# Means of the LayerNorms around the FFN: subtracted from the data, or taken out of w1, w2 and w3 once

## The chip, the cores and the metric

The kernel runs on one core of a Trainium2 chip. The metric is the device time of one execution in microseconds (us); the median of the runs counts. The core has five engines that work side by side, each through its own instructions in order: PE (matrix products, with PEld for its weight loads), DVE (vector), ACT (activations), POOL (GpSimd), and SP, which here only issues DMAs.

## The reference

Sixteen sequences (B) of 512 tokens (S) with 128 features (E) go through an attention block with 16 heads and a gated FFN, each between two LayerNorms without gain and offset:

```python
def _layernorm(x, axis=-1, eps=1e-05):
    m = jnp.mean(x, axis=axis, keepdims=True)
    v = jnp.var(x, axis=axis, keepdims=True)
    return (x - m) / jnp.sqrt(v + eps)

def _L0_ffn_ref(x, w1_w, w1_s, ...):
    # _tlin(x, w, s) = einsum('bsi,oi->bso', x, w) * s
    h = silu(_tlin(x, w1_w, w1_s)) * _tlin(x, w2_w, w2_s)        # 128 -> 512
    h = gelu(_tlin(h, h1_w, h1_s), approximate=False)            # 512 -> 512
    h = gelu(_tlin(h, h2_w, h2_s), approximate=False)            # 512 -> 512
    return _tlin(h, w3_w, w3_s)                                  # 512 -> 128

x = L0_attn_x
x = x + _layernorm(_L0_attn_ref(_layernorm(x), ...))
x = x + _layernorm(_L0_ffn_ref(_layernorm(x), ...))
```

In the attention a head's logits are its scores q q^T times a coefficient that depends on whether two tokens fall into the same hash bucket; then softmax and the product with v follow. All data are float32.

## The kernel before

The kernel is written as many small generators (`prep`, `gather`, `scores`, `coeffs`, `logits`, `softmax`, `attend`, `residual`, `added`, `ffn`, `weights` and others). Each yields its steps with an engine, an estimated cost and a rank. A planner, `Order`, plays them through a clock of its own before anything runs: whenever an engine is free there, it takes the ready step with the lowest rank and emits its instructions. What comes out is one fixed order for each engine. A step that is added, removed or priced otherwise can therefore change the order of everything after it. Scores have rank 0 on PE, av and transposes 1, projections 2, the FFN's products 4, so the FFN fills what attention leaves. Buffers are handed out by counted pools: three PSUM banks for scores, three for the FFN, two for the rest, eleven SBUF buffers for logits, two for x1, one for the transposed input of the FFN.

The unit of attention is a head j of a batch; 256 heads run through one stream. For each head:

- SP issues gathers of `ql`, `qr` (the queries as sums of bfloat16 parts) and `bb` (buckets, broadcast).
- For each of four tiles of 128 tokens PE makes scores `sp` (L881), DVE makes the coefficients `co` (L899) and multiplies the two into `l`, with the row maximum into `mxpad` (L934).
- The maxima of two heads go through a DVE transpose (`mt`), DRAM (`md`) and a broadcast (`mb`); POOL subtracts `mb` from `l` (L991, 128x2048), ACT takes the exponential (L996). Five early heads (`BY_ROWS`) do this on ACT and PE instead.
- After four heads `attend` makes their `av` products on PE (L1056), ACT evicts them (`avs`), PE transposes (`op`, L1077), DVE divides (`rd`, `o`).

When the 16 heads of batch b are done, `added` normalizes `o` into `x1 = x + LN(o)`, `norm_transposed` normalizes and transposes x1 into `xnt_f`, and `ffn` runs four layers: `w` (products with w1 and w2, L1208; silu on ACT, product `h` on DVE), two layers `hp` (L1252; gelu on ACT), and `yp` (L1290). `ffn` ends with LN of `yp` and adds x1. FFN(b) may begin when FFN(b-1) has finished its first hp layer. The last batch is handled in two halves of two tiles.

`moments` makes the two numbers that a LayerNorm needs per token, `rs = (var + eps)^-0.5` and `nm = -mean * rs`; `rescale` then writes `rs * x + nm` on ACT, one instruction for each of four tiles. It is used with name o, f and y in every batch:

- for o and f: DVE `bn_stats` and `bn_aggr` (L438, L442), ACT adds eps (`ve`, L458), POOL takes the power (`rs`, L469), DVE makes `nm`, one instruction on 128x1 for each tile (`negate`, L477);
- for y, whose source is PSUM: ACT copies each tile of `yp` to `y` with the sum in an accumulator (L402), the PSUM bank is handed back, ACT squares with the sum as bias and sums again (L412), then the same ve, rs and nm.

`weights` loads w2, w3, w1, h1, h2 with DMAs issued from ACT; w2 and w3 are multiplied by their scales on POOL, the others' scales are loaded by SP and used later by ACT. `activity` fills PE with products of a zero tile (L1396) until the first FFN begins. The inputs' own LayerNorm (name a, and `inputs`) is not touched.

Of the kernel before, what the change touches and what calls it, by code (L numbers as in the profile page):

```python
# [13 lines left out]
F32 = mybir.dt.float32  # L14
# [176 lines left out]
def tile_lsh_attention_ffn(  # L191
# [77 lines left out]
    ident = const.tile([P, P], F32, name="ident")  # L269
    make_identity(nc, ident)  # L270

    mhalf = const.tile([P, B, NT], F32, name="mhalf")
    nc.gpsimd.memset(mhalf, -0.5)
    eps = const.tile([P, 1], F32, name="eps")
    nc.gpsimd.memset(eps, EPS)
    eps3 = const.tile([P, 1], F32, name="eps3")
    nc.gpsimd.memset(eps3, EPS / E**3)

    junk = const.tile([P, E], BF16, name="junk")
    still = const.tile([P, P], BF16, name="still")  # L280
# [58 lines left out]
    def dve(cost, rank, emit):  # L339
        return ("op", "DVE", cost, emit, rank, None)  # L340

    def act(cost, rank, emit, table=None):
        return ("op", "ACT", cost, emit, rank, table)
# [7 lines left out]
    def get(kind):  # L351
        return ("get", kind)
# [34 lines left out]
    def pairs(tiles):  # L387
        return [tiles[i : i + 2] for i in range(0, len(tiles), 2)]

    def moments(src, name, rank, tiles, copy=None):  # L390


        q, n, t0 = name[0], len(tiles), tiles[0]
        rs = p2.tile([P, NT], F32, tag=f"rs{q}", name=f"rs_{name}_{t0}")
        nm = p2.tile([P, NT], F32, tag=f"nm{q}", name=f"nm_{name}_{t0}")
        if copy is not None:

            sums = p2.tile([P, 2, NT], F32, tag=f"su{q}", name=f"su_{name}_{t0}")

            def sum_(ts_):  # L400
                for t in ts_:
                    nc.scalar.activation(  # L402
                        copy[0][:, t, :],
                        src[:, t, :],
                        AF.Identity,
                        scale=ROOT / E,
                        accum_out=sums[:, 0, t : t + 1],
                    )

            def square(ts_):  # L410
                for t in ts_:
                    nc.scalar.activation(  # L412
                        junk,
                        src[:, t, :],
                        AF.Square,
                        scale=-1.0 * E,
                        bias=sums[:, 0, t : t + 1],
                        accum_out=sums[:, 1, t : t + 1],
                    )

            for ts_ in pairs(tiles):
                yield act(1.0, -2, lambda ts_=ts_: sum_(ts_))
            src = copy[0]
            copy[1]()
            for i, ts_ in enumerate(pairs(tiles)):
                if i:
                    od.loose()
                yield act(1.2, -2, lambda ts_=ts_: square(ts_))
            mean, var = sums[:, 0, :], sums[:, 1, :]
            factor, sign = float(E) ** -3, -1.0 / E  # L430
        else:
            st = p2.tile(
                [P, NT, nc.vector.BN_STATS_DIM], F32, tag=f"st{q}", name=f"st_{name}_{t0}"
            )

            def stats(ts_):
                for t in ts_:
                    nc.vector.bn_stats(st[:, t, :], src[:, t, :])  # L438

            def aggr():  # L440
                for t in tiles:
                    nc.vector.bn_aggr(mv[:, t, :], st[:, t, :])  # L442

            for i, ts_ in enumerate(pairs(tiles)):
                if i:
                    od.loose()
                yield dve(0.46, rank, lambda ts_=ts_: stats(ts_))
            mv = p2.tile(
                [P, NT, nc.vector.BN_AGGR_DIM], F32, tag=f"mv{q}", name=f"mv_{name}_{t0}"
            )  # L450
            yield dve(0.175 * n, rank, aggr)
            mean, var, sign, factor = mv[:, :, 0], mv[:, :, 1], -1.0, 1.0
        ve = p2.tile([P, NT], F32, tag=f"ve{q}", name=f"ve_{name}_{t0}")
        span = slice(t0, t0 + n)
        yield act(
            0.22,
            -5,
            lambda: nc.scalar.activation(  # L458
                ve[:, span],
                var[:, span],  # L460
                AF.Identity,
                bias=eps if factor == 1.0 else eps3,
                scale=factor,
            ),
        )
        yield pool(
            0.37 + 0.16 * n,
            0,
            lambda: nc.gpsimd.tensor_tensor(  # L469
                rs[:, span], ve[:, span], mhalf[:, 0, 0:n], op=ALU.pow  # L470
            ),
        )

        def negate():

            for t in tiles:
                nc.vector.tensor_scalar(  # L477
                    nm[:, t : t + 1],
                    mean[:, t : t + 1],
                    sign,  # L480
                    rs[:, t : t + 1],
                    op0=ALU.mult,
                    op1=ALU.mult,
                )

        yield dve(0.07 * n, rank, negate)
        return nm, rs

    def rescale(src, dst, scales, tiles):

        nm, rs = scales

        def emit(ts_):
            for t in ts_:
                nc.scalar.activation(
                    dst(t),
                    src[:, t, :],
                    AF.Identity,
                    bias=nm[:, t : t + 1],
                    scale=rs[:, t : t + 1],  # L500
                )

        for ts_ in pairs(tiles):
            yield act(0.88, -2, lambda ts_=ts_: emit(ts_))
# [18 lines left out]
            halved[name] = p2.tile([P, NT, E], F32, tag=tag, name=name, bufs=1)  # L523
        return halved[name]

    def norm_transposed(src, xnt, name, rank, tiles):

        xn = shared(f"xn{name[0]}", f"xn_{name}")
        scales = yield from moments(src, name, rank, tiles)
        yield from rescale(src, lambda t: xn[:, t, :], scales, tiles)  # L530
        k = yield get(banks)
        yield from turned(xn, xnt, k, bank(k, f"tp_{name}_{tiles[0]}"), tiles)
# [589 lines left out]
    def added(b, tiles, o, xt, x1, k1, xnt, kx, hs):  # L1122
        scales = yield from moments(o, f"o{b}", 1, tiles)
        kb = yield get(banks)
        ybt = bank(kb, f"yb_{b}_{tiles[0]}").rearrange("p (t e) -> p t e", t=NT)
        yield from rescale(o, lambda t: ybt[:, t, :], scales, tiles)
        span = slice(tiles[0], tiles[-1] + 1)
        yield dve(
            0.1 + 0.125 * len(tiles),
            1,  # L1130
            lambda: nc.vector.tensor_tensor(
                x1[:, span], ybt[:, span], xt[:, span], op=ALU.add
            ),
        )
        od.put(banks, kb)
        yield from norm_transposed(x1, xnt, f"f{b}", 1, tiles)
        od.spawn(ffn(b, tiles, x1, k1, xnt, kx, hs))

    def ffn(b, tiles, x1, k1, xnt, kx, hs):
# [161 lines left out]
        if whole:  # L1301
# [7 lines left out]
            1,  # L1309
            tiles,  # L1310
            (y, lambda: od.put(ffn_banks, kb)),
        )
        kn = yield get(banks)
        ybt = bank(kn, f"yn_{b}_{tiles[0]}").rearrange("p (t e) -> p t e", t=NT)
# [20 lines left out]
    def weights():  # L1335


        for layer, (src, scale, nk, n, name) in enumerate((
            (w2_t, w2_s, 1, HID, "w2"),
            (w3_t, w3_s, NC, E, "w3"),  # L1340
            (w1_t, w1_s, 1, HID, "w1"),
            (h1_t, h1_s, NC, HID, "h1"),
            (h2_t, h2_s, NC, HID, "h2"),
        )):
# [9 lines left out]
            if name in ("w2", "w3"):  # L1354
                if name == "w2":
                    kl = yield get(logit_bufs)
                    sc = p1.tile([P, NT, S], F32, tag=kl, name="scale2")[:, 0, :]
                else:
                    sc = const.tile([P, E], F32, name="scale3")
                yield act(  # L1360
                    0.42,
                    LATE,
                    lambda: nc.scalar.dma_start(out=sc, in_=scale.partition_broadcast(P)),
                )
                yield ("rest", 6.0)
                yield pool(
                    nk * n / 420,
                    2,
                    lambda: nc.gpsimd.tensor_tensor(
                        w, w, sc.unsqueeze(1).to_broadcast([P, nk, n]), op=ALU.mult  # L1370
                    ),
                )
                if name == "w2":
                    od.put(logit_bufs, kl)
            else:
                w_sb[name + "s"] = sc = const.tile([P, NC], F32, name=name + "s")
                yield dma(
                    2,
                    2,
                    lambda: nc.sync.dma_start(  # L1380
                        out=sc,
                        in_=scale.rearrange("(c p) -> p c", p=P),
                        allow_slow_non_contiguous=True,
                    ),
                    cost=0.6,
                )
        od.set(loaded)

    def activity():
# [76 lines left out]
```

## Time and profile before

| | before |
|---|---|
| median of 3 runs | 1368.63 us (1368.58 to 1369.19) |
| the profiled execution: its time, its span | 1371.57 us, 1369.8 us |
| instructions | 21290 |
| mean granted clock of PE | 0.989 |
| MB read from and written to HBM | 153.50, 19.13 |
| subtraction on POOL, 128x2048 | 251 times, 4566 ns |
| l on DVE, 128x512 | 1024 times, 680 ns |
| nm_f, nm_y on DVE, 128x1 | 64 times each, 204 and 204 ns |
| hp on PE, 128x512 float32 | 960 records, 596 ns (two records for one product) |

An instruction's recorded duration can overlap the next one's on the same engine, so what an instruction costs a full engine is the distance from its start to the next start. Busy time is the union of the durations. In the groups of waits, "X <- Y: us, times, longest" is idle time of X that ended when Y was done. In the chain of work that ended last, each line is a start, a duration and what ran.

### The profile page before, as it was taken

Reading aid. Unit: us, or ns where it says so; the run is one execution under the profiler, and the core shown is the slowest. Engines: PE = TensorE matmul, PEld = TensorE weight load, DVE = VectorE, ACT = ScalarE, POOL = GpSimd, SP = SyncE. Lnnn points to the kernel's source line nnn. Section 1 sums busy time; section 2 is a strip of 40 time slices with the busy share of each in tenths; the row PEclk is TensorE's granted clock in tenths of the full one; section 3 lists DMA queues with packets and bytes.
Section 4 is the critical chain, followed back from the end, with each engine's and each line's share of the span. In section 5 each row is a group of like instructions: output and inputs, shape, how many; then the busy total and the mean of one; then the engine's idle time right before and its main releaser. Section 6 shows DMA issues by size and latency. Waiting matters only on the chain.

```text
span 1369.8 us, 21290 instructions
## 1 busy us (share of the span) xinstructions
PE 1316.2 (96%) x6008; PEld 568.3 (41%) x6008; DVE 1234.5 (90%) x3992; ACT 1143.8 (84%) x1665; POOL 1197.4 (87%) x317
## 2 busy tenths in 40 slices
PE   9999999999999999999999999999999999999997
PEld 3344334334443443434344344433443343433466
DVE  4999999799998999999999999999999999999220
ACT  2688888889898898889989798988979898888953
POOL 1398989999899998999989999998999999899810
PEclk9999999899999999999999999999999999999999
DMA  4645454444544545454444545554445545443100
GB/s 135 189 140 154 131 151 138 135 129 134 154 113 128 131 133 142 132 142 134 132 123 128 141 133 144 132 143 116 146 124 139 141 132 140 122 122 116 47 8 8
DMA packets 158867, 174.04 MB, mean 127 GB/s; under 512 B 33821, under 2 KB 117277, under 8 KB 158749
## 3 DMA queue, kind: packets, MB, share of 16 engines
q1 hardware_dynamic: 155937, 169.20, 44.3%
q10 hardware_dynamic: 2811, 3.48, 0.8%
q8 instruction: 48, 0.79, 0.2%
q14 instruction: 71, 0.57, 0.2%
HBM read 153.50 MB, written 19.13 MB: 126 GB/s over the span
## 4 chain that ended last, share of the span: by engine, by line
PE 57%; DVE 24%; POOL 6%; issue 6%; DMA 4%; ACT 3%; SPq 0%; ACTq 0%; POOLq 0%; DVEq 0%
PE hp L1252 25%; PE av L1056 13%; DVE l L934 12%; PE sp L881 10%; DVE co L899 8%; POOL l L991 6%; PE w L1208 3%; DMA mb<-md 2%; PE yp L1290 2%; PE op L1077 2%; DMA bb<-bkd 1%; ACT l L996 1%; PE vp L794 1%; PE activity L1396 1%; DVE h L1178 1%
## 5 line engine op out<-in xcount | busy, mean ns | idle before, releaser
L991 POOL TENSOR_TENSOR l<-l,mb 128x2048 f32<-128x2048 f32 x251 | 1135.6, 4566 | 56.8 <-DMA mb<-md 41.5
L934 DVE CUSTOM_DVE_ANT_0 l<-co,sp 128x512 f32<-128x512 bf16 x1024 | 662.4, 680 | 14.5 <-PE av L1056 11.0
L996 ACT ACTIVATE l<-l 128x2048 f32<-128x2048 f32 x251 | 477.8, 1907 | 23.3 <-POOL l L991 22.1
L1252 PE MATMUL hp<-h,h 128*128 128x512 f32 (+1 forms) x1088 | 494.3, 570 | 0.1
L899 DVE TENSOR_SCALAR co<-bb,bj 128x516 bf16<-128x516 bf16 x1024 | 451.7, 471 | 2.8 <-DMA bb<-bkd 2.8
L881 PE MATMUL sp<-qr,ql 72*128 72x512 bf16 x1024 | 357.8, 384 | 35.6 <-DVE mxpad L934 31.8
L1252 PEld LDWEIGHTS hp<-h,h 128*128 128x128 f32 x1088 | 201.4, 190 | 160.3 <-issue 137.7
L1056 PE MATMUL av<-l,vaug 128*32 128x512 f32 x2008 | 265.1, 605 | 0.0
L881 PEld LDWEIGHTS <-ql 72*128 72x128 bf16 x1024 | 94.6, 98 | 331.8 <-issue 309.6
L1208 PE MATMUL w<-xnt_f,w 128*128 128x512 f32 (+1 forms) x272 | 133.1, 585 | 4.3 <-ACT a L1196 2.6
L996 ACT ACT_TABLE_LOAD x87 | 111.6, 1283 | 1.5
L1056 PEld LDWEIGHTS av<-l,vaug 128*32 128x32 f32 x2008 | 45.7, 109 | 116.6 <-issue 85.2
L1396 PE MATMUL activity<-still 128*128 128x512 bf16 x328 | 88.8, 387 | 1.0 <-DVE still L281 1.0
L934 DVE DVE_READ_ACCUMULATOR2_ANT mxpad<- 128x1 f32 x1004 | 83.0, 83 | 0.0
L1070 ACT COPY avs<-av 128x512 f32<-128x512 f32 x64 | 37.4, 584 | 48.3 <-PE av L1056 48.2
L1266 ACT ACT_TABLE_LOAD x59 | 75.7, 1283 | 1.0
L1208 PEld LDWEIGHTS w<-xnt_f,w 128*128 128x128 f32 x272 | 50.9, 195 | 51.1 <-issue 20.8
L1178 DVE TENSOR_TENSOR h<-w,a 128x512 f32<-128x512 f32 (+1 forms) x68 | 44.2, 656 | 29.4 <-PE w L1208 18.9
L1290 PEld LDWEIGHTS yp<-w,h 128*128 128x128 f32 x512 | 65.7, 193 | 11.3 <-issue 6.7
L1290 PE MATMUL yp<-w,h 128*128 128x128 f32 x512 | 66.5, 277 | 0.0
L469 POOL TENSOR_TENSOR rs_y<-ve_y,mhalf 128x4 f32<-128x4 f32 (+1 forms) x17 | 16.7, 985 | 48.4 <-ACT ve_y L458 47.8
L1266 ACT ACTIVATE h<-hp,h1s 128x512 f32<-128x512 f32 (+1 forms) x68 | 41.8, 660 | 14.9 <-PE hp L1252 14.5
(102 smaller groups left out, 1008.4 us busy)
## 6 DMA issues: line engine op xcount, KB each, us to landing
mb<-md SPq DMA_DIRECT2D x251, 256.0 KB
bb<-bkd SPq DMA_DIRECT2D x256, 130.5 KB
ql<-qd SPq DMA_DIRECT2D x256, 72.0 KB
qr<-qd SPq DMA_DIRECT2D x255, 72.0 KB
qd<-q SPq DMA_DIRECT2D x96, 128.0 KB
xta<-in_L_attn_x_dram SPq DMA_DIRECT2D x16, 256.0 KB
xtr<-in_L_attn_x_dram SPq DMA_DIRECT2D x16, 256.0 KB
xtm<-in_L_attn_x_dram SPq DMA_DIRECT2D x15, 256.0 KB
```

Source lines behind the costliest of these rows:

```text
L881: nc.tensor.matmul(sp, lhsT=ql[:, ts(t, P)], rhs=qr, start=True, stop=True)
L899: nc.vector.tensor_scalar(co, bb.rearrange("p (r c) -> p r c", c=BP)[:, :, 0:BC], bjs[b][:, c : c + 1], float(NBKT - 2), op0=ALU.is_equal, ...
L934: nc.vector.tensor_tensor_reduce(out=l, in0=co[:, 0:S], in1=sp, scale=1.0, scalar=-3.0e38, op0=ALU.mult, op1=ALU.max, accum_out=mx[:, t : ...
L991: lambda: nc.gpsimd.tensor_tensor(l, l, mb.unsqueeze(1).to_broadcast([P, NT, S]), op=ALU.subtract),
L996: yield act(1.82, 0, lambda: nc.scalar.activation(l, l, AF.Exp, scale=SCALE), "exp")
L1056: nc.tensor.matmul(av[k * Q : (k + 1) * Q, :], lhsT=va[:, t, c : c + Q], rhs=ls[gg * GH + k][0][:, t, :], start=(t == 0), stop=(t == NT - 1),)
L1178: lambda: nc.vector.tensor_tensor(h[:, c, cols], g2, a, op=ALU.mult),
L1208: lambda: nc.tensor.matmul(gp, lhsT=w_sb[which][:, 0, ts(c, P)], rhs=xnt[:, cols], start=True, stop=True),
L1252: lambda i=i: nc.tensor.matmul(hp, lhsT=w[:, i, ts(c, P)], rhs=hin[:, i, cols], start=(i == 0), stop=(i == NC - 1),),
L1266: nc.scalar.activation(h[:, c, cols], hp, AF.Gelu, scale=sc[:, c : c + 1])
L1290: nc.tensor.matmul(yp[:, ts(t, E)], lhsT=h[:, i, ts(t, P)], rhs=w_sb["w3"][:, i, :], start=(i == 0), stop=(i == NC - 1),)
L1396: nc.tensor.matmul(bk, lhsT=still, rhs=still.unsqueeze(1).to_broadcast([P, NT, P]), start=start, stop=stop,)
```

## The change

A LayerNorm's mean is constant over a token's 128 features. Subtracting it from the input of w1 and w2 is the same as subtracting, from each column of the two weights, that column's mean over the 128 input features. Subtracting it from the output of w3 is the same as subtracting, from each row of w3, its mean over the 128 output features. The change does this with the weights once:

- `centering` = identity - 1/128. After w2 is scaled and after w1 is loaded, PE multiplies each by it into an FFN bank (`c_w2`, `c_w1`) and ACT copies the result back over the weight.
- w3: DVE sums its rows (`sums3`), scales the sums by -1/E, and ACT adds them as a bias, chunk by chunk.
- w1 is loaded before w3 instead of after it; `centering` and w3's scale share one buffer.
- `moments` has a flag `free`, set for f and y: nm is neither allocated nor made, and `rescale` has bias 0.0. For f the statistics are made as before, mean included, since the variance needs it.
- for y, whose mean is now zero, the four copies with sums become one copy of all tiles, and the squares have no bias; `ve` uses 1/E and eps instead of scaled ones.

```diff
+    centering = p1.tile([P, P], F32, tag="w3", name="centering")
+    nc.vector.tensor_scalar(centering, ident, -1.0 / E, None, op0=ALU.add)
...
-    eps3 = const.tile([P, 1], F32, name="eps3")
-    nc.gpsimd.memset(eps3, EPS / E**3)
...
-    def moments(src, name, rank, tiles, copy=None):
+    def moments(src, name, rank, tiles, copy=None, free=False):
...
-        nm = p2.tile([P, NT], F32, tag=f"nm{q}", name=f"nm_{name}_{t0}")
+        if not free:
+            nm = p2.tile([P, NT], F32, tag=f"nm{q}", name=f"nm_{name}_{t0}")
         if copy is not None:
-            sums = p2.tile([P, 2, NT], F32, tag=f"su{q}", name=f"su_{name}_{t0}")
-            def sum_(ts_):
-                for t in ts_:
-                    nc.scalar.activation(copy[0][:, t, :], src[:, t, :], AF.Identity,
-                        scale=ROOT / E, accum_out=sums[:, 0, t : t + 1])
+            var = p2.tile([P, NT], F32, tag=f"su{q}", name=f"su_{name}_{t0}")
+            mean, factor, sign = None, 1.0 / E, None
             def square(ts_):
                 for t in ts_:
-                    nc.scalar.activation(junk, src[:, t, :], AF.Square, scale=-1.0 * E,
-                        bias=sums[:, 0, t : t + 1], accum_out=sums[:, 1, t : t + 1])
+                    nc.scalar.activation(
+                        junk, copy[0][:, t, :], AF.Square, accum_out=var[:, t : t + 1]
+                    )
-            for ts_ in pairs(tiles):
-                yield act(1.0, -2, lambda ts_=ts_: sum_(ts_))
-            src = copy[0]
+            whole = slice(t0, t0 + n)
+            yield act(
+                0.12 + 0.1 * n, -2, lambda: nc.scalar.copy(copy[0][:, whole], src[:, whole])
+            )
...
+        if free:
+            return None, rs
         def negate():
...
-                    bias=nm[:, t : t + 1],
+                    bias=0.0 if nm is None else nm[:, t : t + 1],
...
-        yield from norm_transposed(x1, xnt, f"f{b}", 1, tiles)
+        yield from norm_transposed(x1, xnt, f"f{b}", 1, tiles, free=True)
...
             (w2_t, w2_s, 1, HID, "w2"),
+            (w1_t, w1_s, 1, HID, "w1"),
             (w3_t, w3_s, NC, E, "w3"),
-            (w1_t, w1_s, 1, HID, "w1"),
...
-                    sc = const.tile([P, E], F32, name="scale3")
+                    sc = p1.tile([P, E], F32, tag="w3", name="scale3")
...
+                else:
+                    sums = const.tile([P, nk], F32, name="sums3")
+                    yield dve(0.6, 2, lambda: nc.vector.reduce_sum(sums, w, axis=AX.X))
+                    yield dve(0.1, 2, lambda: nc.vector.tensor_scalar(
+                        sums, sums, -1.0 / E, None, op0=ALU.mult))
+                    for i in range(nk):
+                        yield act(0.35, LATE, lambda: nc.scalar.activation(
+                            w[:, i], w[:, i], AF.Identity, bias=sums[:, i : i + 1]))
...
+            if nk == 1:
+                kb = yield get(ffn_banks)
+                cp = bank(kb, f"c_{name}")
+                yield pe(1.2, 3, lambda: nc.tensor.matmul(
+                    cp, lhsT=centering, rhs=w[:, 0, :], start=True, stop=True))
+                yield act(0.6, LATE, lambda: nc.scalar.copy(w[:, 0, :], cp))
+                od.put(ffn_banks, kb)
```

More of the change, by code (lines that the diff above doesn't have):

```diff
@@ L388, in pairs @@
         return [tiles[i : i + 2] for i in range(0, len(tiles), 2)]
-    def moments(src, name, rank, tiles, copy=None):
+    def moments(src, name, rank, tiles, copy=None, free=False):
         q, n, t0 = name[0], len(tiles), tiles[0]
         rs = p2.tile([P, NT], F32, tag=f"rs{q}", name=f"rs_{name}_{t0}")
-        nm = p2.tile([P, NT], F32, tag=f"nm{q}", name=f"nm_{name}_{t0}")
+        if not free:
+            nm = p2.tile([P, NT], F32, tag=f"nm{q}", name=f"nm_{name}_{t0}")
         if copy is not None:
-            sums = p2.tile([P, 2, NT], F32, tag=f"su{q}", name=f"su_{name}_{t0}")
-            def sum_(ts_):
-                for t in ts_:
[L402 to L408, printed above, removed]
+            var = p2.tile([P, NT], F32, tag=f"su{q}", name=f"su_{name}_{t0}")
+            mean, factor, sign = None, 1.0 / E, None
             def square(ts_):
@@ L412, in square @@
                     nc.scalar.activation(
[L413 to L418, printed above, removed]
-                    )
-            for ts_ in pairs(tiles):
-                yield act(1.0, -2, lambda ts_=ts_: sum_(ts_))
-            src = copy[0]
+                        junk, copy[0][:, t, :], AF.Square, accum_out=var[:, t : t + 1]
+                    )
+            whole = slice(t0, t0 + n)
+            yield act(
+                0.12 + 0.1 * n, -2, lambda: nc.scalar.copy(copy[0][:, whole], src[:, whole])
+            )
             copy[1]()
@@ L428, in moments @@
                 yield act(1.2, -2, lambda ts_=ts_: square(ts_))
-            mean, var = sums[:, 0, :], sums[:, 1, :]
-            factor, sign = float(E) ** -3, -1.0 / E
         else:
@@ L461, in moments @@
                 AF.Identity,
-                bias=eps if factor == 1.0 else eps3,
+                bias=eps,
                 scale=factor,
@@ L524, in shared, with norm_transposed @@
         return halved[name]
-    def norm_transposed(src, xnt, name, rank, tiles):
+    def norm_transposed(src, xnt, name, rank, tiles, free=False):
         xn = shared(f"xn{name[0]}", f"xn_{name}")
-        scales = yield from moments(src, name, rank, tiles)
+        scales = yield from moments(src, name, rank, tiles, free=free)
         yield from rescale(src, lambda t: xn[:, t, :], scales, tiles)
@@ L1311, in ffn @@
             (y, lambda: od.put(ffn_banks, kb)),
+            free=True,
         )
@@ L1374, in weights @@
                     od.put(logit_bufs, kl)
+                else:
+                    sums = const.tile([P, nk], F32, name="sums3")
+                    yield dve(0.6, 2, lambda: nc.vector.reduce_sum(sums, w, axis=AX.X))
+                    yield dve(
+                        0.1,
+                        2,
+                        lambda: nc.vector.tensor_scalar(sums, sums, -1.0 / E, None, op0=ALU.mult),
+                    )
+                    for i in range(nk):
+                        yield act(
+                            0.35,
+                            LATE,
+                            lambda: nc.scalar.activation(
+                                w[:, i], w[:, i], AF.Identity, bias=sums[:, i : i + 1]
+                            ),
+                        )
             else:
@@ L1386, in weights @@
                 )
+            if nk == 1:
+                kb = yield get(ffn_banks)
+                cp = bank(kb, f"c_{name}")
+                yield pe(
+                    1.2,
+                    3,
+                    lambda: nc.tensor.matmul(
+                        cp, lhsT=centering, rhs=w[:, 0, :], start=True, stop=True
+                    ),
+                )
+                yield act(0.6, LATE, lambda: nc.scalar.copy(w[:, 0, :], cp))
+                od.put(ffn_banks, kb)
         od.set(loaded)
```

## Prediction

> **What bounds the kernel now.** I read the page first, then the busy time by stretch, then the waits of each engine inside the steady stretch, and last the chain at the end. The page's first part:
>
> ```profile
> PE 1316.2 (96%) x6008; PEld 568.3 (41%) x6008; DVE 1234.5 (90%) x3992; ACT 1143.8 (84%) x1665; POOL 1197.4 (87%) x317
> ```
>
> These are averages over three stages: a start of some 130 us without FFN work, a long middle of like batches, and an end of some 75 us with FFN work alone. The busy time by stretch separates the middle (450 to 1240 us, ten batches) from the end:
>
> ```profile
> 450.00:1240.00 790.00, 770.39 (x3482) 321.34 (x3479) 775.79 (x2510) 689.52 (x859) 762.18 (x194) 1.00 0.48 134
> 1296.00:1370.00 74.00, 65.03 (x307) 46.95 (x305) 10.68 (x47) 35.84 (x93) 5.13 (x7) 0.97 0.02 8
> ```
>
> The columns are PE, PEld, DVE, ACT, POOL, then clock and DMA. In the middle DVE is busy 98%, POOL 96.5%, PE 97.5%, ACT 87%: three engines are within two per cent of each other. The waits in the same stretch say who waits for whom (total us, times, longest):
>
> ```profile
> PE sp L881 <- DVE mxpad L934: 17.6, 50, 1.0
> ```
> ```profile
> POOL rs_f L469 <- DVE mxpad L934: 9.1, 3, 3.4
> POOL rs_f L469 <- ACT ve_f L458: 6.3, 3, 2.8
> ```
> ```profile
> DVE rd L1087 <- PE op L1077: 8.6, 11, 1.4
> ```
>
> PE waits for DVE twice as long as DVE waits for PE; POOL waits for the statistics that pass through DVE and ACT. So DVE sets the pace of attention by a narrow margin. The powers of the o-statistics start at 132.49 us (batch 0) and 1238.21 us (batch 14): 79.0 us a batch.
>
> Is PE really nearly full? Its starts answer better than its busy share: in the timeline four hp records from 462.62 are followed by sp at 464.34, so 0.43 us each with nothing between; sp takes 0.22. Per batch 64 hp records, 16 w, 64 sp, four av groups at 3.6 us, yp, transposes and projections sum to about 73 us of the 79, and the changes between sp and av cost some 3 more. The chain at the end:
>
> ```profile
> 1276.24 4.57 POOL l L991
> ...
> 1286.70 13.74 PE hp L1252 x32
> 1300.44 3.57 PE av L1056 x32
> ...
> 1330.53 27.89 PE hp L1252 x128
> 1358.43 3.58 PE yp L1290 x32
> ```
>
> POOL ends its last subtraction at 1295.2 (timeline: two from 1286.22, 9.01 together); after that the last av (1300.4) and 58 us of PE almost without a hole follow, then 7.8 us of the last LayerNorm and its write. What is still queued on PE behind the last av is therefore paid in full.
>
> A rule speaks for a larger gain than I forecast. The Trainium skill, Perfetto Trace Analysis, section Identifying the Most-Contended Engine, takes occupancy for Vector, Scalar and GpSimd, judges TensorE by MFU and LDWEIGHTS busy share instead of matmul share, and says to optimize the most-contended engine first. By it PE (41% in weight loads) has much room, DVE binds alone, and the change would give the whole 13.7 us worked out below, about 1354.9. The starts 0.43 us apart say that PE has little room, and I go by them.
>
> **The change part by part.** The sum is made on the profiled execution: 1371.57 us, span 1369.8, 1.8 outside it; the median of the runs is 1368.63, 2.9 lower. I carry the difference over to the median.
>
> *DVE, removed:* per batch two groups of four nm operations (f and y; o keeps its own). The timeline shows what one costs when DVE is full:
>
> ```profile
> 705.64 0.68 DVE L934 CUSTOM_DVE_ANT_0 l<-co,sp 128x512 f32<-128x512 bf16 x1
> 706.24 0.08 DVE L934 DVE_READ_ACCUMULATOR2_ANT mxpad<- 128x1 f32 x1
> 706.24 0.58 DVE L477 TENSOR_SCALAR nm_f<-mv_f,rs_f 128x1 f32<-128x1 f32 x4
> 706.73 0.47 DVE L899 TENSOR_SCALAR co<-bb,bj 128x516 bf16<-128x516 bf16 x1
> ```
>
> Four take 0.58 recorded but hold the engine 0.49 (706.24 to 706.73), so 0.98 a batch; 14 batches lie before the last o: 13.7 us on the engine that paces. This is the upper end of the gain. The lower end is what the new order itself shows: when the av of head group 60 (of 64) starts, the built program has 510.8 us of FFN products (0.86 a product of 512 columns) behind it instead of 516.9, so at least 6.1 us of PE work leave the attention stage. POOL must follow: it idles 27.8 us of the 790, and 15.4 of that is the rs_f wait above, which a shorter DVE queue shortens. DVE being the fullest, I stand nearer the upper end: 11 us.
>
> *ACT:* per batch four Identity with accumulator from yp become one copy. They start 0.25 to 0.26 us apart (1324.15, .42, .67, .92), 1.0 in all; a 128x512 copy from PSUM takes 0.58 (the avs row). 0.4 us less on an engine 87% busy: hidden by POOL and DVE, at nothing. If ACT were full it would be 6 us. The squares and rescales keep their count. The f and y chains lose a hop through DVE; both are hidden by PE's queued work except for the very last y, below.
>
> *Start:* centering (one 128x128 DVE operation) stands while DVE waits for POOL's power: nothing. PE gets c_w2 between the first transposes and qp, which opens the chain to the first gathers:
>
> ```profile
> 10.47 1.95 PE L644 MATMUL qp<-xnt_a,wq_sb 128*128 128x512 f32 x2 [0.22 <-ACT xnt_a L515]
> ```
>
> c_w2 has qp's shape; it takes the place of one activity product (0.43), so qp is 0.4 (0.86 at full pitch) to 1.5 us late (qp's own 1.95): I take 1.5, the row of the same moment. w1s on SP goes between two qd writes, in a hole of 0.4 us. The eviction of c_w1 (0.58) and three w3 loads stand on ACT ahead of the first qr issue; behind them wait the first scores. In return three h1 loads (256 KB each) leave the place where the first bb landed slowly (5.92 us from 21.24 in the chain): at the 204 to 228 GB/s of that stretch the 768 KB are up to 3.6 us of traffic. They go behind w3's additions and meet the first mb instead, for which POOL waits there anyway (20.67 us before 41.45). w3's sums are one reduction over 128x512 and one small operation on DVE, 0.26 (block) to 0.68 (x) plus 0.2, taken 0.8, standing ahead of head 0's last l and waiting for POOL's scaling of w3; four bias additions (0.48 each) on an idle ACT. Together -3 to +4 us; the terms I can price cancel: 0.
>
> *End:* the order of the built program shows what the quicker attention leaves over. Behind the last av stand 29 hp products of 512 columns instead of 16, all else equal: 13 x 0.86 = 11.2 us. Between the last sp and the last av PE has 19.7 us of work instead of 25.7. From POOL's end to the kernel's end before: 1369.8 - 1295.2 = 74.6. After: 3.5 to the last av (exp 1.9, its table load and hand-overs), 3.6 av, 67.2 queued products (56.0 + 11.2), 0.5 of stalls, and 7.1 for the last y (7.8 less 0.6 for nm and its wait, less 0.15 for copy against two sums): 81.9, so +7.3.
>
> *Sum:* 0 - 11 + 7.3 = -3.7: profiled 1367.9, median 1364.9.
>
> **The rivals.** *PE takes all of it.* Three engines at 96 to 98%: the FFN put off in the middle is done at the end, the total of PE's work is unchanged (two small products more), and only its idle time can shrink. For it: the back-to-back starts and a chain that is 57% PE. Against: the 17.6 us in which sp waits for DVE, which should shrink. Attention 7.3 us quicker, end 7.3 longer: 1368.6.
>
> *The end wins.* The 13 extra products behind the last av cost 7.3 us; this decides as soon as POOL's last subtraction comes less than 7.3 us earlier than 1295.2. POOL runs almost without a hole from 1200 to 1295, and its waits before that are for DMA and ACT as well; if those stay and only 3 us come off, the time is 1368.6 - 3 + 7.3 = 1372.9.
>
> *Start.* The later qp and the crowded first mb give +4 with everything else as forecast: 1368.9, inside the first rival. That the change does not do what it says I exclude: the built program has 24 rows that write nm on DVE instead of 58.
>
> **How the numbers follow.** Forecast 0.47 (1357 to 1365.9), no change 0.22, end wins 0.31. About 0.2% (2.7 us) is what a measurement of this kernel tells from no change; the forecast's band lies under it, so faster 0.47, same 0.22, slower 0.31. Ends of the range: -13.7 - 3 + 5 = -11.7, 1357; -6.1 + 4 + 8.5 = +6.4, 1375. The 5 and 8.5 are the end term with an av that comes 2.3 us before or 1.2 us after my placing.
>
> **What would show it.** Right: rs_o of batch 14 starts 8 to 13 us before 1238.21; sp's wait for DVE under 17.6 in the same ten batches; POOL's last l ends near 1284; from there 80 to 84 us to the end, with hp between the two last av groups fewer and behind them more. Wrong: a batch period of still 79 us (then DVE did not pace); POOL's end before 1280 (then PE had more room than its starts say); a first co much off 27.26 us (then the start decides); a granted clock unlike that of before, which was 0.92 between 212 and 293 us and 1.00 from 450 to 1240, since PE has little room to make up for it.

## The result, and the profile after

The changed kernel took 1379.24 us (median of 4 runs, 1377.11 to 1381.8), the kernel before 1368.91 beside it: a ratio of 1.0072 (95% interval 1.0052 to 1.0093), so about 10 us slower. 1364.9 was forecast, with 1357 to 1375 around it. The profiled execution took 1379.33 us with a span of 1377.5 (before 1369.8): 7.7 us are to be found in the traces. The rest of the 10 is scatter: the traced execution before is 2.7 us over its median. It is one of the late ones, with its first FFN product w at 154.2 us. Six traces whose order up to there is that of before (this one and five of the runs below) have it between 151.0 and 154.9.

The first part of the page after, and the busy time of the same two stages as before (PE, PEld, DVE, ACT, POOL, then granted clock, DMA share and GB/s):

```profile
PE 1323.3 (96%) x6014; PEld 572.2 (42%) x6014; DVE 1222.3 (89%) x3867; ACT 1121.1 (81%) x1560; POOL 1197.3 (87%) x316
```
```profile
450.00:1240.00 790.00, 768.12 (x3446) 318.78 (x3445) 763.76 (x2414) 668.33 (x783) 760.68 (x193) 0.99 0.49 133
1296.00:1378.00 82.00, 73.77 (x325) 50.16 (x323) 9.91 (x36) 36.09 (x85) 5.12 (x7) 0.97 0.04 14
```

The operations are gone as announced: DVE has 125 instructions less, ACT 105. In the middle DVE is busy 12.0 us less and PE 2.3 us less, at a clock of 0.99 instead of 1.00. All three engines that were nearly full are now less full, and the kernel is slower: somebody waits more. From the first FFN product to the last l, before (154.2 to 1271.2) and after (156.0 to 1271.8), the busy times are:

```profile
154.20:1271.20 1117.00, 1081.96 (x4855) 447.44 (x4855) 1086.03 (x3503) 979.73 (x1294) 1071.30 (x269) 0.99 0.48 133
156.00:1271.80 1115.80, 1079.12 (x4823) 444.67 (x4823) 1072.55 (x3385) 955.51 (x1200) 1076.40 (x271) 0.98 0.49 133
```

The waits of DVE in these stretches, before and then after; each line is us, times, longest:

```profile
DVE l L934 <- PE av L1056: 11.0, 6, 3.3
DVE rd L1087 <- PE op L1077: 10.1, 16, 1.4
DVE h L1178 <- PE w L1208: 3.1, 6, 1.3
DVE l L934 <- PE sp L881: 2.8, 8, 0.8
```
```profile
DVE l L924 <- PE av L1046: 13.8, 12, 3.2
DVE rd L1077 <- PE op L1067: 10.7, 14, 1.5
DVE l L924 <- PE sp L871: 9.7, 20, 1.6
DVE h L1168 <- PE w L1198: 4.0, 5, 2.6
```

With the lines under 1 us the sums are 28.2 and 39.1. That closes the account of the engine that paced: from first w to last l it is 1117.0 us before and 1115.8 after; without waits 1088.8 and 1076.7, so 12.1 us less work. (By the rows above it is 13.5 less busy and 12.3 more idle; the list leaves out the shortest waits.) That 12.1 is near the 13.7 computed is partly luck, because three pairs of co and l, some 3 us, now lie ahead of the first w. But 10.9 of it came back as waiting, nearly all of it for scores, av and w on PE, and the first w was 1.8 us later, less than the 3.9 over which it scatters. The last l therefore ends 0.6 us later than before (1271.8), where the forecast wanted it 11 earlier.

In the steady stretch the waits that the prediction named stand so:

```profile
PE sp L871 <- DVE mxpad L924: 18.7, 42, 1.1
...
POOL l L981 <- DMA mb<-md: 16.4, 12, 2.8
...
POOL rs_f L456 <- ACT ve_f L445: 2.1, 1, 2.1
```

PE's wait for DVE did not shrink (17.6 before). POOL's 15.4 us for the statistics of f are nearly gone (2.1), but it waits 16.4 us for the broadcast maxima mb instead of 3.9, and is idle 29.3 us of the 790 instead of 27.8. POOL ends 19.0 us behind the last l instead of 24.0: at 1290.8 instead of 1295.2. The end follows in the chain that ended last:

```profile
1289.81 1.28 ACT L1186
1291.85 2.07 PE w L1198 x2
1293.92 3.24 PE hp L1242 x6
1297.16 3.57 PE av L1046 x32
...
1339.15 26.33 PE hp L1242 x122
...
1368.70 1.76 PE yp L1280 x12
```

From POOL's end to the end of the span it is 86.7 us, 12.2 more than before (74.5). So the 7.7 us are, but for rounding: +0.6 at the last l, -5.0 from there to POOL's end, +12.2 behind it.

### The profile page after: what moved, and what is told of

Its sections match the earlier page's. It is cut to its first block, busy times and chain, and to the rows that moved or that the text cites. A ratio compares the mean times of both kernels' runs of the same rounds, so it can differ in the third digit from the quotient of the medians.

```text
span 1377.5 us, 21072 instructions
## 1 busy us (share of the span) xinstructions
PE 1323.3 (96%) x6014; PEld 572.2 (42%) x6014; DVE 1222.3 (89%) x3867; ACT 1121.1 (81%) x1560; POOL 1197.3 (87%) x316
## 4 chain that ended last, share of the span: by engine, by line
PE 71%; DVE 18%; DMA 3%; issue 3%; ACT 3%; SPq 1%; POOL 0%; POOLq 0%; ACTq 0%; DVEq 0%
PE hp L1242 27%; PE av L1046 16%; PE sp L871 13%; DVE l L924 9%; DVE co L889 6%; PE w L1198 5%; PE yp L1280 4%; PE activity L1417 2%; DMA bb<-bkd 2%; PE op L1067 1%; PE qp L634 1%; PE vp L784 1%; PE pp L673 1%; DVE mxpad L924 1%; DMA xta<-in_L_attn_x_dram 0%
## 5 line engine op out<-in xcount | busy, mean ns | idle before, releaser
L924 DVE CUSTOM_DVE_ANT_0 l<-co,sp 128x512 f32<-128x512 bf16 x1024 | 663.4, 678 | 26.8 <-PE av L1046 13.8
L1198 PE MATMUL w<-xnt_f,w 128*128 128x512 f32 (+1 forms) x272 | 138.1, 601 | 4.1 <-ACT a L1186 3.7
L1280 PEld LDWEIGHTS yp<-w,h 128*128 128x128 f32 x512 | 67.2, 196 | 16.6 <-issue 12.0
```

The lines of the kernel that those rows point to most:

```text
L924: nc.vector.tensor_tensor_reduce(out=l, in0=co[:, 0:S], in1=sp, scale=1.0, scalar=-3.0e38, op0=ALU.mult, op1=ALU.max, accum_out=mx[:, t : ...
L1198: lambda: nc.tensor.matmul(gp, lhsT=w_sb[which][:, 0, ts(c, P)], rhs=xnt[:, cols], start=True, stop=True),
L1280: nc.tensor.matmul(yp[:, ts(t, E)], lhsT=h[:, i, ts(t, P)], rhs=w_sb["w3"][:, i, :], start=(i == 0), stop=(i == NC - 1),)
```

## The experiments

Theory: DVE paces, and what it gained was lost because the planner dealt out another order, in which PE serves attention later and leaves more FFN to the end. Rivals: the centred weights, or the work of centring them, cost time themselves; PE takes all of it; the granted clock falls with the data.

**Is it the data?** The change in its own order, with nothing centred:

```diff
-  sums, sums, -1.0 / E, None, op0=ALU.mult
+  sums, sums, 0.0, None, op0=ALU.mult
-  cp, lhsT=centering, rhs=w[:, 0, :], ...
+  cp, lhsT=ident, rhs=w[:, 0, :], ...
```

> The changed kernel with the identity in the place of the centering matrix and w3's sums multiplied by 0 instead of -1/E: every instruction stays where it is, but w1 keeps its values -1, 0, 1 and w2 and w3 their scaled ones (the means are subtracted nowhere). Theory D (the denser mantissas of the centred w1 make PE draw more, and the granted clock falls): the clock returns to about 0.989, no reduced stretch between 450 and 1290 us, and the time to 1368 to 1371. Theory O (the new order costs the time, and the clock follows the order or chance): 1377 to 1381, clock near 0.982.

Measured: 1377.86 us, ratio 1.0068 (1.0045 to 1.0090). The same loss, and from 230 us on the stretches of reduced clock begin where the change has them, within 2 us. The other way round, the kernel before with dense numbers in the place of w1, and of h1 and h2:

```diff
- in_=src[i * P : (i + 1) * P, :]
+ in_=x[i].rearrange("(p t) e -> p (t e)", t=NT) if name in ("w1",) else src[...]   # or ("h1", "h2")
```

> The kernel before, with 128x512 numbers of the input x loaded into w1 instead of the ternary weight; order and instructions are those of before. Theory D: reduced clock in the middle as after the change, clock 0.98 to 0.985, time up by 4 to 10 us to 1373 to 1379. Theory O: clock 0.989, time 1368 to 1370.

> The kernel before, with numbers of x loaded into h1 and h2, whose products are four times those of w1 and w2 together: the dose of theory D. Theory D: clock 0.94 to 0.975, time 1385 to 1420. Theory O, or a clock that does not look at data: 1368 to 1371, clock 0.989.

Measured: 1368.33 (0.9996; 0.9985 to 1.0007) and 1368.59 (0.9989; 0.9979 to 0.9999), granted clock 0.990 in both. What the weights hold is worth nothing here.

**What is DVE's relief worth by itself?** The kernel before with nm of f and y not issued and the rescales without bias, while the planner still counts the step, so that the order stays:

```diff
- yield dve(0.07 * n, rank, negate)
+ yield dve(0.07 * n, rank, (lambda: None) if free else negate)
...
-     bias=nm[:, t : t + 1],
+     bias=0.0 if nm is None else nm[:, t : t + 1],
```

> The kernel before with the nm operations of f and y not issued and the rescales without bias, while the planner keeps a step of the same cost in their place, so that every other instruction stands where it stood (the mean of f and y is not subtracted). It measures what 13.7 us less on DVE are worth in an unchanged order. Forecast's view (DVE paces by a narrow margin): 1356 to 1362, POOL's last subtraction 8 to 12 us earlier. Rival (PE takes all of it): 1366 to 1369, with DVE's idle time up by what was removed.

Measured: 1360.91 us, ratio 0.9932 (0.9917 to 0.9946): -9.3 us. The last l ends at 1257.8, 13.4 earlier than in the trace of before. Of this 2.8 us is the first w (151.4 instead of 154.2), which lies within its scatter, and 10.6 is the stretch from there to the last l:

```profile
151.40:1257.80 1106.40, 1076.19 (x4853) 446.01 (x4853) 1075.09 (x3395) 969.27 (x1292) 1070.91 (x270) 0.99 0.48 134
```

In the trace of before, the 27 groups of nm in this stretch hold DVE for 13.4 us, from the first start of a group to the next start behind it. The relief earns 10.6 of them. PE's wait for DVE shrinks as the prediction wanted it of the change, while POOL's waits for the statistics of f stay (17.6 us):

```profile
PE sp L882 <- DVE mxpad L935: 14.1, 35, 1.0
...
POOL rs_f L470 <- DVE mxpad L935: 10.3, 3, 3.5
POOL rs_f L470 <- ACT ve_f L459: 7.3, 3, 3.1
```

The counter-test is to relieve PE instead, by one of the 32 hp products of 512 columns in each whole batch, 12.9 us in all:

```diff
- lambda i=i: nc.tensor.matmul(hp, ...)
+ (lambda: None) if layer == 2 and c == 3 and i == 1 and whole else lambda i=i: nc.tensor.matmul(hp, ...)
```

> The kernel before with one of the 32 hp products of each whole batch left out (layer 2, column block 3, second partial product) while the planner still counts it: 15 x 0.86 = 12.9 us less on PE, every other instruction where it stood. It is the mirror of the run without nm (13.7 us less on DVE gave 8.6 to 9.3). If DVE paces attention (forecast's view): 1366 to 1369, POOL's last subtraction within 3 us of 1295. If PE takes all of it: 1356 to 1361.

Measured: 1366.18, ratio 0.9976 (0.9963 to 0.9990): -3.3 us, a quarter. A later run with 20.6 us less on PE (below) gave nothing. So the kernel before gains far more from relieving DVE than PE; "PE takes all of it" falls.

**Is it the order?** The whole change, but played by the planner as the kernel before: the skipped steps still count at their old prices, and the centring is emitted in one piece behind the last weights step.

```diff
+ for i, ts_ in enumerate(pairs(tiles)):
+     yield act(1.0, -2, (lambda: None) if i else lambda: nc.scalar.copy(...))
...
- if free:
-     return None, rs
...
- yield dve(0.07 * n, rank, negate)
+ yield dve(0.07 * n, rank, (lambda: None) if free else negate)
```

> The whole change, computed as the change does it, but with the planner shown the steps and prices of before (empty steps where something is gone), and the centering of w1, w2 and w3 emitted with the last planned step of the weights: two more products on PE, otherwise before's order. If only the order was wrong (theory O): 1357 to 1363, like the run without nm, one or two us more for the centering or one less for the shorter last y. If the weights' part itself costs what the change lost: over 1368.

Measured: 1361.98 us (6 runs, 1360.76 to 1365.32), ratio 0.9950 (0.9938 to 0.9962). The same arithmetic as the change, 17 us quicker than it, and quicker than both kernels. Its waits of DVE from first w to last l:

```profile
DVE l L924 <- PE av L1046: 12.3, 6, 3.3
DVE rd L1077 <- PE op L1067: 10.9, 18, 1.4
DVE h L1168 <- PE w L1198: 2.1, 6, 0.7
DVE l L924 <- PE sp L871: 1.8, 6, 0.6
```

Together with the small ones 29.1, as before (28.2), where the change has 39.1: the wait for sp is 1.8 instead of 9.7. Behind the last av stand 16 hp products, not 29.

Which part of the change disturbs the order? Its FFN half alone (no nm, one copy of yp; weights as before), and its weights half alone (centred, nm kept):

```diff
 # FFN half: the change without its weights part
-            (w1_t, w1_s, 1, HID, "w1"),          # back behind w3
-                    sums = ...; yield dve(...); yield act(...)
-            if nk == 1:
-                ... c_w1, c_w2
 # weights half: the kernel before, with those lines, nm and the four copies kept
```

> One part of the change, planned: f and y without nm, y with one copy, but w1, w2 and w3 untouched as before (the mean is subtracted nowhere). The built order leaves 32 hp products of 512 columns behind the last av (before 16, after the change 29). Theory O: the end after POOL's last subtraction is 85 to 90 us, the time 1372 to 1384 although DVE has 13.7 us less. If the weights' part had spoiled the change: 1356 to 1362.

> The other part, planned: w1, w2 and w3 centred once as in the change, and nm still made and used as before, so that no work is saved. 25 hp products stand behind the last av. Theory O: 1370 to 1380, mostly in the end and in the places of reduced clock. If only the FFN part's order hurts: 1368 to 1371.

Measured: 1382.78 (1.0104; 1.0089 to 1.0119) and 1386.55 (1.0123; 1.0110 to 1.0136). Each alone loses more than both together (0.7%), and with the order kept both together lose nothing, so neither part carries a cost of that size of its own. The second is over the range that I had expected. The barest form changes no instruction at all, only the price that the planner believes for nm:

```diff
- yield dve(0.07 * n, rank, negate)
+ yield dve(0.1225 * n, rank, negate)
```

> The kernel before with one number of the planner changed: the price of negate, 0.07 us a tile, set to the 0.1225 that the trace shows. Not one instruction more or less, another order; 28 hp products behind the last av. Theory O: the order alone moves the time by some 5 to 12 us, here up, 1372 to 1381. If the order matters little and it was the work: 1367 to 1371.

Measured: 1386.30, ratio 1.0122 (1.0107 to 1.0136). Moving the same instructions about costs 17 us, more than I had expected. The order of the kernel before looks like a fortunate one, and a change that re-deals it loses that. To compare under another order, both kernels got another price for ve:

```diff
- 0.22,
+ 0.285,
```

> The change with one price of the planner altered (ve on ACT 0.285, as the trace has it, instead of 0.22): same instructions, another order, 32 hp products behind the last av. Theory O: 1375 to 1390, from POOL's end to the end 85 to 95 us. If the change's order is no accident but its work: 1377 to 1381.

> The kernel before with the same price altered (ve 0.285 instead of 0.22): same instructions, another order, 32 hp products behind the last av. Theory O: well above before, 1378 to 1392, and above the change with the same price by what DVE saves (5 to 13 us). If before's order is not special: 1367 to 1372.

Measured: the change 1376.10 (1.0038; 1.0026 to 1.0049), the kernel before 1384.04 (1.0096; 1.0079 to 1.0113). Under this price the change is 7.9 us ahead. With the order kept it is 8.0 ahead (against 1370.02 of the kernel before beside it). That the two agree so closely is partly luck, since under the new price each kernel still has an order of its own. But all three re-dealt orders without nm of f and y (the change, its FFN half, and this one: 1376.1 to 1382.8) are quicker than all three with it (the weights half and the kernel before under either price: 1384.0 to 1386.6).

**Can the end be bought back?** The change, with the FFN of batch 12 ranked ahead of av and projections, so that less is left over:

```diff
- 4,
+ (0.5 if 12 <= b < 13 else 4),
```

> The change with one rank altered: the FFN products of batch 12 get 0.5 on PE instead of 4. Up to that batch the order is that of the change; at the end 16 hp products of 512 columns stand behind the last av instead of 29. If the backlog at the end is a cost of the change's order (theory O): the time from POOL's last subtraction to the end falls from 86.7 to 74 to 78 us and the whole to 1367 to 1373. If the backlog does not matter, or comes back as a later POOL: 1377 to 1381.

Measured: 1392.52, ratio 1.0156 (1.0136 to 1.0177), far from the 1367 to 1373 that I had expected. The tail behind POOL is back at 74.8 us, and 16 products stand behind the last av, but attention pays: 16 heads that take 77.2 us in the change took 105.3 (DVE from 1127.2 to 1232.5), with DVE busy 78 of the 105:

```profile
1127.00:1232.00 105.00, 93.60 (x380) 40.50 (x382) 77.97 (x244) 76.74 (x97) 79.99 (x22) 0.90 0.37 101
```
```profile
DVE l L924 <- PE av L1046: 35.4, 13, 21.6
```

One wait for av is 21.6 us long. The backlog was moved, not removed: done as one block it stands in front of av, done at the end it is paid behind POOL.

**What halves the clock?** In the change 41.0 us between the first w and the last yp run at a granted clock of 0.50 (before 23.9), in pieces of 3.4 or 6.8 us; the kernel before has none between 431 and 1365, the change five there. Most pieces begin behind a stretch of 3.4 us in which PE had less than half its fill of products (counts in the last section). Around 885 us of the change, the busy time by stretch:

```profile
882.05:885.45 3.40, 1.79 (x8) 0.86 (x8) 3.40 (x13) 2.93 (x5) 3.40 (x2) 1.00 0.04 9
885.50:892.30 6.80, 5.97 (x12) 2.75 (x12) 5.66 (x19) 4.80 (x5) 6.80 (x3) 0.50 0.53 157
```

And its timeline of PE (start, us, operation, in brackets the idle time and who ended it):

```profile
884.32 0.38 PE L871 MATMUL sp<-qr,ql 72*128 72x512 bf16 x1 [1.10 <-DVE mxpad L924]
...
887.30 1.91 PE L1198 MATMUL w<-xnt_f,w 128*128 128x512 f32 x2
889.00 1.91 PE L634 MATMUL qp<-xnt_a,wq_sb 128*128 128x512 f32 x2
890.71 1.06 PE L871 MATMUL sp<-qr,ql 72*128 72x512 bf16 x2
```

No FFN product stands between the sp there, so PE waits for DVE (1.10 us) and is busy 1.79 of 3.40. Right behind, w and qp take 1.70 from start to start instead of 0.86, and DVE waits 1.14 us for the sp behind them before its next l (891.38). To see whether the hole is the cause or only stands beside the dip: 24 of the 32 hp products of FFN(8) are left out of the kernel before, at a place without a dip, against 24 products spread over twelve batches:

```diff
- lambda i=i: nc.tensor.matmul(hp, ..., stop=(i == NC - 1))
+ (lambda: None) if whole and b == 8 and i else lambda i=i: nc.tensor.matmul(
+     hp, ..., stop=(i == NC - 1 or (whole and b == 8)))
# spread: (lambda: None) if whole and 2 <= b < 14 and layer == 2 and c == 3 and i in (1, 2) else ...
```

> The kernel before, its order kept, with 24 of the 32 products of FFN(8)'s two hidden layers left out (of each four that are summed only the first is made): 24 x 0.86 = 20.6 us of PE work missing in one place, between that batch's w (801 us before) and its yp (878 us). The output of batch 8 is therefore not the reference's. Theory W (windows of 3.41 us in which PE runs at most half full are what halves the granted clock next): the share of PE falls to about 0.6 there, single windows to under 0.5, and one or more stretches at clock 0.50, each a multiple of 3.41 us long, begin behind such windows between 824 and 878 us, where the kernel before has none from 427.1 to 1365.7; products inside are 0.85 instead of 0.43 a record. Time: 20.6 us of PE relief at the rate of the run with 15 products less (3.3 us for 12.9) is -5.3, less 2 to 5 us for each dip: 1364 to 1372. Rival (the clock falls for a reason that lies elsewhere in the order or in the time since the start): no dip there, clock 1.00 from 450 to 1240 as before, and about 1364.

> The kernel before, its order kept, with the same number of products left out, 24, but two in each of the twelve batches 2 to 13 (layer 2, last column group, second and third of the four that are summed): the outputs of these batches are not the reference's. 1.7 us of PE work missing in one place at a time. Theory W: single windows lose 1.7 of 3.41 us only where PE would have been full, so few or no new stretches at clock 0.50 between 450 and 1240 (none to two); time by the rate of the run with 15 products less, 0.256 x 20.6 = -5.3: about 1364. Rival (the amount of PE work in the whole kernel moves the clock): the reduced clock is as long as in the kernel with the 24 products left out in one batch. If DVE paces alone and PE's relief is worth nothing, 1368 to 1369 in both.

Measured: with the hole in one place three dips appear where the kernel before has none, at 829.7 (3.4 us), 846.7 (10.2) and 867.2 (6.8); the holes spread out give none between 427 and 1279, but one at 1279.9 (3.4 us), where the kernel before has none either. The kernel with the hole, then the kernel before, in the same stretches:

```profile
820.00:880.00 60.00, 49.32 (x218) 15.97 (x215) 58.74 (x196) 52.86 (x57) 60.00 (x16) 0.83 0.52 134
843.30:846.70 3.40, 1.03 (x3) 0.19 (x2) 3.40 (x15) 2.43 (x3) 3.40 (x2) 1.00 0.82 244
846.75:856.95 10.20, 8.53 (x17) 2.49 (x20) 10.20 (x35) 7.79 (x10) 10.20 (x4) 0.50 0.37 100
```
```profile
820.00:880.00 60.00, 59.22 (x267) 23.17 (x264) 58.99 (x196) 53.06 (x57) 60.00 (x16) 1.00 0.50 134
```

PE is busy 1.03 of 3.40 us, and then the clock is 0.50. So a hole in one place makes dips. The times are 1369.01 (ratio 1.0002; 0.9992 to 1.0011) and 1368.65 (0.9999; 0.9990 to 1.0008): the dips cost nothing that the times show, and DVE ran full through them (58.74 of 60). 20.6 us less on PE earn nothing either. The -5.3 that I expected of the spread holes, by the rate of the run with 15 products less, did not come. In its trace the stretch from first w to last l is 1113.7 us, against 1115.5 to 1117.0 in three traces of the order before with nothing left out (the kernel before and the two with dense weights), but behind POOL's end stand 76.1 us instead of 74.5, with the dip at 1279.9 ahead of it. Between a quarter and nothing, what PE's relief is worth stays open.

## Why the prediction was wrong, point by point

- *DVE, removed, 13.7 us:* the amount was right. With the order kept it earned 10.6 us between first w and last l, and 9.3 of the time, so the 11 would have been about right in the old order. *DVE paces by a narrow margin* is right too, against the rival in which PE takes all: 20.6 us less on PE earned nothing. Its reason was weaker than I read it: in those ten batches DVE's waits for PE sum to 12.5 us, of which I had counted the largest group (8.6), so PE waited 1.4 times as long and not twice.
- *"I stand nearer the upper end: 11 us"* is the step that failed. It sized what attention gains by DVE's work, and priced the new order at nothing but its end. I held the 6.1 us of PE work that leaves the stage for a lower bound; it was none. In the new order DVE waits 10.9 us more for PE, and the last l came 0.6 us late. The batch period (rs_o of batch 0 at 135.18, of batch 14 at 1243.35) stayed at 79.2 us. I had written that a period of 79 would mean that DVE did not pace; that inference was wrong as well: the same relief in the old order shortened it from 79.0 to 78.2. A pace can stay because the pacing engine is given new waits. Why the new order serves scores and av later at each place is not shown beyond the dips below.
- *"POOL must follow"*, since a shorter DVE queue would shorten its wait for rs_f: not so. In the old order that wait stayed (17.6 us after 15.4). In the change it went with the order, and the wait for mb took its place.
- *The clock:* I had named a granted clock unlike before's as what would make the forecast wrong, but put no price on it. The extra dips come from holes in PE, and these from where the FFN products stand. By DVE's gaps from 4 us ahead of a dip to 10 us behind it, 20.7 us of its idle time lie near dips after, 13.8 before: at most 6.9 of the 10.9 are of this kind. How much of that the slower clock costs and how much the hole that caused it would have cost anyway, no run here separates.
- *Start, 0:* +1.8 at the first w, inside the -3 to +4, and less than the 3.9 over which the first w scatters. The first co, a sign that I had named, came 3.5 earlier (23.80 instead of 27.26), near the 3.6 of traffic that had left its way. Its l then waited 2.1 us for sp and began at 27.55, where the six traces mentioned have 26.6 to 28.9: the start does not decide.
- *End, +7.3:* the 29 products were right, and the sum too small by 4.8. The last av starts 6.4 us after POOL's end instead of 3.5, with a dip at 1291.7 on the way (w took 2.07 for its two records in the chain above). From the end of av to the end of the last yp it is 69.7 us instead of 67.2 + 0.5, and 7.0 after that, as forecast (7.1).
- *The end wins,* the rival at 0.31, had the right sign, place and condition (POOL's end less than 7.3 earlier: it was 4.4), at 1372.9. It missed the size of the end.
- *The rule by occupancy* (Trainium skill, Perfetto Trace Analysis, section Identifying the Most-Contended Engine), which by my reading gave 1354.9: with the order kept, relieving the most-contended engine did earn 9.3 us, though not the whole 13.7. For the change as built the rule is as wrong as my forecast, because it speaks of instructions and not of their order.

## What to carry to other kernels

Where a planner deals out one fixed order, an edit has two effects, its instructions and a new order, and here the second (price alone: +17 us) was larger than the first (-8 to -9 us): build a version that keeps the old order, and compare both kernels under several orders before judging an edit. In the profile, ask of a relieved engine not only how much less it works but whom it will wait for next; list its waits over the whole stage, since DVE's busy share moved from 90 to 89% while its waits grew by 11 us. Keep filler work spread over the stretch where the matrix engine waits for others: done as one block ahead of attention it cost 21.6 us in one wait, and a hole that left PE under half full for some 3 us was mostly followed by half the clock.

## What the runs showed of the hardware

The granted clock drops to 0.50 for one to three times 3.4 us behind a stretch of 3.41 us, aligned with the dips, in which PE's products fill less than half. Counting each record at its full-speed pitch (hp 0.43 us, sp 0.22), such stretches outside of dips were followed by a dip in 5 of 7 cases before, 6 of 7 after, 8 of 9 with the hole in one place, out of some 340 stretches per trace; 0 to 3 dips in a trace followed a fuller one, so the rule is not exact. In the dip, fp32 products of 512 columns start 0.85 us a record apart instead of 0.43. The Trainium skill, TensorE: Matmul & The Clock Gate, Part 1, gives a free-running window of 3413 ns, half rate after an idle one; length and rate agree with these rows, but the window need not be idle: 1.79 of 3.40 us busy was enough. Dense in place of ternary weights did not move the clock (0.990 and 0.990).
